# Row transfers on GpSimd without the memsets between them: a routed feed-forward, state-space, routed feed-forward layer on one core

## The chip, the core and the metric

The kernel runs on one core of a Trainium2 chip. Time is device microseconds for one execution. Before the change three runs took 1312.5, 1317.1 and 1319.66 us, with a median of 1317.1 us. The profile is of one further execution, which took 1298.57 us; its span from the first to the last instruction is 1296.8 us, at a mean granted TensorE clock of 0.887.

## What is computed

The input is 2 sequences of 2048 rows of 128 numbers, in float32. Three residual steps follow each other, each on a layer-normalised copy of the rows:

```python
x = x + 0.5 * ffn(layernorm(x))    # 32 experts, 4 per row, plus a shared part
x = x + attn(layernorm(x))         # a state-space scan over the 2048 rows
x = x + 0.5 * ffn(layernorm(x))    # the same experts again
```

In `ffn` a softmax over 32 logits picks the 4 best experts of each row. The row goes through those 4 (`down(silu(gate(row)) * up(row))`, all 128 x 128), the results are added with the weights of the softmax, and a shared block of the same form with 512 hidden units is added. In `attn` a state of 256 x 16 numbers per sequence is carried over the rows by `h = h * exp(dt * A) + dt * u * B`, and read out with `C`.

## The kernel before, in words

**Blocks and groups.** The 4096 rows are 8 blocks of 512. The first `ffn` treats the blocks in groups of 1, 1, 2 and 4 blocks, the last one in groups of 4, 2, 1 and 1 (`GROUPS`). The state-space part treats one block after another. One order of all operations mixes the three parts: state-space work of early blocks runs beside `ffn` work of other groups.

**Rows to their experts and back.** For a group, `mixture` works out a place for each (row, expert) pair, so that rows of one expert stand together. Then GpSimd sends the rows there: one indirect transfer (L916, 128 rows of 512 bytes) per tile of 128 rows and chosen expert, 16 for each block, from SBUF to a table `xs` in DRAM. SyncE loads the table in pieces of 4 x 128 rows (L1006) with the weights of their experts (L1018 or L1048); TensorE, ScalarE and VectorE apply the expert (L1066 to L1113), and the results go to a table `ys` in DRAM (L1117). GpSimd fetches them back by 4 indirect transfers for each tile (L1197) into one of the 4 buffers `yg`. ScalarE writes the weights on diagonals `dg` (L1222), TensorE adds the four up with them (`sum`, L1230), and VectorE adds the sum to `x` (L1241). Over all, 256 transfers go out (L916) and 256 come back (L1197).

**GpSimd's other work.** In the state-space part it makes the driving term of every state by one multiplication of 128 x 1024 (`hst`, L1456, 128 of them, into a ring of 4 buffers), which VectorE then scans (L1494), and three smaller operations for each half block (L1424 to L1426).

**What sets the order.** `ORDER` is a list of operation numbers written out by hand; `Plan.run` (L279) lists the operations in it and `Plan.emit` (L307) writes them out. PE, DVE, ACT and SP keep this order as it stands. GpSimd's instructions are tied by edges without a wait (`pool`, L394): everything but an outgoing transfer is tied to what went before; outgoing transfers are tied to the last instruction that is not one, and not to each other.

**The pad.** `Plan.run` counts how many transfers follow each other among GpSimd's operations (`row`; transfers are those with a `lag`). For the third and every later one of such a row it sets `o.pause`, and `emit` then writes a memset of a tile `pad`, which nobody reads, ahead of the transfer. The pad counts as an instruction that is not an outgoing transfer, so it also ties the transfers around it in order.

```python
    def pool(made, scatter=False):
        ins = made.ins
        if scatter:
            if behind[0] is not None:
                edge(behind[0], ins)
            behind[1].append(ins)
        else:
            for a in behind[1] or ([behind[0]] if behind[0] is not None else []):
                edge(a, ins)
            behind[0], behind[1] = ins, []
        return ins
    pad = const.tile([P, 256], BF16, tag="pad", name="pad")
    def pause():
        pool(nc.gpsimd.memset(pad, 0.0))
```

**Semaphores.** Each transfer on GpSimd signals its landing on one of eight semaphores in turn, so the ninth waits for the landing of the first.

Of the kernel before, what the change touches and what calls it, by code (L numbers as in the profile page):

```python
# [245 lines left out]
class Plan:  # L246
# [32 lines left out]
    def run(self):  # L279
        order, done, row = [], set(), 0  # L280
        for part in ORDER.split():
            first, _, last = part.partition("-")
            order += [self.ops[i] for i in range(int(first), int(last or first) + 1)]
        assert len(order) == len(self.ops)
        for o in order:


            assert o.deps <= done
            for b in o.bufs:
                if b.made:  # L290
                    continue
                line = self.made[b.ring]
                assert b.place is None or b.place == len(line)
                assert b.follow is None or (
                    b.follow.made and self.made[b.follow.ring][len(line)] is b.follow
                )
                k = len(line) - self.rings[b.ring]
                assert k < 0 or done.issuperset(line[k].ops)
                b.made = True
                line.append(b)  # L300
            done.add(o)
            if o.eng == "pool":
                row = row + 1 if o.lag else 0
                o.pause = row > 2
        return order

    def emit(self, order, pause):  # L307
# [1348 lines left out]
```

## Time and profile before

| what | value |
|---|---|
| median of 3 runs | 1317.1 us (1312.5 to 1319.66) |
| profiled execution | 1298.57 us, span 1296.8 us |
| PE matmul / weight loads busy | 977.2 us (75%) / 775.3 us (60%) |
| GpSimd busy | 976.6 us (75%), 1043 instructions |
| DVE / ACT busy | 822.4 us (63%) / 785.6 us (61%) |
| transfers out (L916) | 256, mean 0.975 to 0.989 us |
| DMA, mean | 175 GB/s |

The busy time of a GpSimd transfer is not the time in which its data move; that is done by the DMA engines afterwards. The row "software_dynamic" of the DMA queues holds these transfers: 16384 packets, 33.59 MB, that is 32 packets for each of the 512. An idle time that ends with "issue" is one for which the profile shows no wait.

### The profile page before, as it was taken

What the parts mean: (1) busy time and instruction counts of PE and PEld (TensorE: products, weight loads), DVE (VectorE), ACT (ScalarE), POOL (GpSimd) and SP (SyncE); (2) the same over time, 40 slices, a digit from 0 to 9 for tenths busy, and PEclk for the clock granted to TensorE, in tenths of its full rate; (3) what the DMA queues carried; (4) which work ended last, traced back from release to release, by engine and by line L of the source; (5) the groups of instructions that cost most, each with busy time, mean ns of one, the idle gap of its engine ahead of it and who ended that gap; (6) DMA issues with size and microseconds to landing.
All of it is one profiled execution on the core that took longest, in us unless ns stands there. A gap on an engine that the chain in (4) does not pass through costs nothing. (4 is left out here: it accounts for less than half of the span.)

```text
span 1296.8 us, 19377 instructions
## 1 busy us (share of the span) xinstructions
PE 977.2 (75%) x5823; PEld 775.3 (60%) x5848; DVE 822.4 (63%) x1643; ACT 785.6 (61%) x1532; POOL 976.6 (75%) x1043
## 2 busy tenths in 40 slices
PE   3778864778898978878668756767887889667776
PEld 2456654566777766565545445545767877666664
DVE  7543451146576999898989999998688633212221
ACT  4324333477789999677879735775678546333342
POOL 3874678088869685888989889989876867477586
PEclk9978987889999999777889776888999989879888
DMA  9768875678978464222232212332798968668632
GB/s 320 237 189 261 276 211 162 201 226 285 292 246 247 152 171 142 85 64 69 81 81 73 76 49 82 98 115 90 226 277 250 310 206 234 177 179 226 173 92 68
DMA packets 253514, 226.87 MB, mean 175 GB/s; under 512 B 24513, under 2 KB 218690, under 8 KB 253378
## 3 DMA queue, kind: packets, MB, share of 16 engines
q1 hardware_dynamic: 236994, 191.67, 48.6%
q0 software_dynamic: 16384, 33.59, 8.9%
q8 instruction: 60, 0.98, 0.3%
q14 instruction: 76, 0.62, 0.2%
HBM read 154.65 MB, written 70.52 MB: 174 GB/s over the span
## 5 line engine op out<-in xcount | busy, mean ns | idle before, releaser
L1456 POOL TENSOR_TENSOR hst<-dtu,bs 128x1024 f32<-128x1024 f32 x128 | 302.7, 2370 | 56.0 <-PE y L1271 15.9
L1197 POOL DMA_INDIRECT yg<-ys,idx x256 | 248.0, 969 | 114.5 <-PE sum L1230 52.1
L1076 PE MATMUL gu<-xT,wt 128*128 128x128 f32 x1536 | 220.3, 296 | 57.9 <-issue 13.6
L1076 PEld LDWEIGHTS gu<-xT,wt 128*128 128x128 f32 x1536 | 203.0, 207 | 93.6 <-issue 44.2
L916 POOL DMA_INDIRECT xs<-xn,idx x192 | 189.9, 989 | 88.8 <-issue 33.8
L1494 DVE TENSOR_TENSOR_SCAN hst<-da,st,hst 128x512 f32<-128x512 f32 x192 | 240.1, 1272 | 14.2 <-POOL hst L1456 5.9
L1094 DVE TENSOR_TENSOR h<-sgq,gu 128x256 f32<-128x256 f32 x192 | 77.9, 418 | 227.5 <-ACT sgq L1088 129.6
L1468 ACT ACTIVATE da<-dt,a 128x512 f32<-128x512 f32 x256 | 175.0, 690 | 73.2 <-DVE hst L1494 66.3
L1271 PEld LDWEIGHTS y<-ident,hst 128*128 128x128 f32 x1024 | 135.1, 157 | 77.0 <-issue 52.1
L1088 ACT ACTIVATE sgq<-gu 128x256 f32<-128x256 f32 x192 | 71.3, 384 | 162.9 <-PE gu L1076 81.7
L415 ACT ACT_TABLE_LOAD x130 | 166.8, 1283 | 4.1 <-PEq L1644 0.8
L1271 PE MATMUL y<-ident,hst 128*128 128x128 f32 x1024 | 152.3, 299 | 19.5 <-DVE hst L1507 18.1
L1507 DVE TENSOR_TENSOR hst<-hst,c 128x1024 f32<-128x1024 f32 x128 | 154.9, 1210 | 11.3 <-PE c L1480 3.6
L1104 PE MATMUL oq<-wt,h 128*128 128x128 f32 x768 | 110.4, 290 | 38.7 <-DVE h L1094 19.2
L1104 PEld LDWEIGHTS oq<-wt,h 128*128 128x128 f32 x768 | 100.2, 201 | 55.2 <-DVE h L1094 22.2
L409 POOL MEMSET pad<- 128x256 bf16 x336 | 110.5, 329 | 0.3
L1113 ACT COPY yq<-oq 128x512 f32<-128x512 f32 x96 | 55.7, 586 | 79.0 <-PE oq L1104 34.5
L1480 PE MATMUL c<-cm,pick 128*128 128x512 bf16 x103 | 44.4, 432 | 77.7 <-DVE hst L1507 72.6
L1230 PEld LDWEIGHTS sum<-yg,dg 128*128 128x128 f32 x512 | 71.6, 210 | 34.7 <-issue 12.9
L1230 PE MATMUL sum<-yg,dg 128*128 128x128 f32 x512 | 77.8, 300 | 17.3 <-issue 7.5
L1069 ACT COPY xT<-pt_x 128x512 f32<-128x512 f32 x96 | 55.7, 585 | 54.6 <-PE pt_x L1066 21.8
L1222 ACT ACTIVATE dg<-ident,wk 128x128 f32<-128x128 f32 x256 | 81.0, 394 | 10.4 <-PE sum L1230 10.4
(154 smaller groups left out, 1531.6 us busy)
## 6 DMA issues: line engine op xcount, KB each, us to landing
wt<-w_dram SPq DMA_DIRECT2D x256, 192.0 KB
bs<-bd SPq DMA_DIRECT2D x128, 256.0 KB
xs<-xs SPq DMA_DIRECT2D x96, 256.0 KB
ys<-yq SPq DMA_DIRECT2D x96, 256.0 KB
xs<-zero SPq DMA_DIRECT2D x52, 256.0 KB
wt<-in_gate_w SPq DMA_DIRECT2D x64, 128.0 KB
wt<-in_up_w SPq DMA_DIRECT2D x64, 128.0 KB
wt<-in_down_w SPq DMA_DIRECT2D x64, 128.0 KB
```

Source lines behind the costliest of these rows:

```text
L409: pool(nc.gpsimd.memset(pad, 0.0))
L415: nc.scalar.preload_act_table_set(name)
L916: nc.gpsimd.indirect_dma_start(out=xs_b.t, out_offset=bass.IndirectOffsetOnAxis(ap=route["idx"][:, i * TB + t, k : k + 1], axis=0), in_=xn ...
L1076: nc.tensor.matmul(gu.t[:, j, s, :], wt.t[:, s, j * H : (j + 1) * H], xT.t[:, s0 + s, :], start=True, stop=True,)
L1104: nc.tensor.matmul(o.t[:, s, :], h.t[:, s, :], wts[s // 2].t[:, s % 2, 2 * H :], start=True, stop=True,)
L1197: nc.gpsimd.indirect_dma_start(out=yg.t[:, k, :], out_offset=None, in_=ys_b.t, in_offset=bass.IndirectOffsetOnAxis(ap=route["idx"][:, i * ...
L1230: nc.tensor.matmul(sm_.t, dg.t[:, k, :], yg.t[:, k, :], start=(k == 0), stop=(k == TOPK - 1),)
L1271: nc.tensor.matmul(y[:, t, k * P : (k + 1) * P], src[:, k, t * P : (t + 1) * P], ident.t, is_transpose=True, start=start and k == 0 and t ...
L1456: nc.gpsimd.tensor_tensor(h.t[:, :, 1:], dtu.t, bs.t.unsqueeze(1).to_broadcast([P, ND, T]), ALU.mult)
L1468: nc.scalar.activation(da.t, dt.t[:, k, :], AF.Exp, scale=a_t.t[:, k, s : s + 1])
L1494: nc.vector.tensor_tensor_scan(h.t[:, k, 1:], da.t, h.t[:, k, 1:], 0.0 if ini else st_sb[:, k, s : s + 1], ALU.mult, ALU.add,)
L1507: nc.vector.tensor_tensor(h.t[:, :, :T], h.t[:, :, 1:], cb.t.unsqueeze(1).to_broadcast([P, ND, T]), ALU.mult,)
```

## The change

The third and later transfers of a row get no pad any more. Nothing else of the source is touched:

```diff
             if o.eng == "pool":
                 row = row + 1 if o.lag else 0
-                o.pause = row > 2
+                o.pause = False
         return order
```

336 memsets of 128 x 256 bf16 go. The instructions of the other four engines stay, in the same order. On GpSimd the sequence of the remaining instructions stays too, with two exceptions, both where outgoing transfers are no longer tied by a pad: nine of the four-block group now stand ahead of the branch of an earlier group (L1139) and not behind it, and among three transfers of two late groups one has moved to the front.

## The prediction

> **What bounds the kernel now.** I read the page first: engines, then groups.
>
> ```profile
> PE 977.2 (75%) x5823; PEld 775.3 (60%) x5848; DVE 822.4 (63%) x1643; ACT 785.6 (61%) x1532; POOL 976.6 (75%) x1043
> ...
> L1456 POOL TENSOR_TENSOR hst<-dtu,bs 128x1024 f32<-128x1024 f32 x128 | 302.7, 2370 | 56.0 <-PE y L1271 15.9
> L1197 POOL DMA_INDIRECT yg<-ys,idx x256 | 248.0, 969 | 114.5 <-PE sum L1230 52.1
> ...
> L916 POOL DMA_INDIRECT xs<-xn,idx x192 | 189.9, 989 | 88.8 <-issue 33.8
> ...
> L409 POOL MEMSET pad<- 128x256 bf16 x336 | 110.5, 329 | 0.3
> ```
>
> No engine is full. GpSimd's 977 us hold 110.5 us of pads, and the reader should notice the idle column: transfers have much, pads none. The windows by stage (columns: busy time and count of each engine, clock, DMA share, GB/s) show why the mean misleads.
>
> ```profile
> 20.00:230.00 210.00, 144.59 (x767) 108.34 (x765) 92.20 (x370) 74.35 (x151) 150.79 (x230) 0.87 0.73 231
> 230.00:1000.00 770.00, 602.79 (x3535) 469.54 (x3559) 631.96 (x976) 575.28 (x1057) 616.81 (x485) 0.89 0.50 152
> 1000.00:1297.00 297.00, 223.84 (x1503) 193.29 (x1503) 85.67 (x227) 127.99 (x305) 206.69 (x310) 0.90 0.65 186
> ```
>
> In the middle DVE (632 of 770) and GpSimd (617) hand the scan buffers to each other; at both ends PE, DMA and transfers alternate. Counted in GpSimd's timeline, 114, 73 and 149 pads lie in these three stages. Then the view of waits (columns: sum in us, times, longest), first GpSimd's, then SyncE's own:
>
> ```profile
> POOL yg L1197 <- PE sum L1230: 52.1, 17, 15.1
> ...
> POOL xs L916 <- ACTq L1139: 23.8, 1, 23.8
> ```
>
> ```profile
> SPq L1006 <- DMA xs<-xn,idx: 23.8, 2, 14.3
> ```
>
> So returning transfers wait 52.1 us for a free `yg`, and one outgoing group waits 23.8 us: slack that hides slower or faster transfers. But SyncE waits 23.8 us for rows to land, in two places (9.6 us near 45 us, and 14.3 us late in the middle): there transfers are on the path. Last, GpSimd's timeline of one row of transfers:
>
> ```profile
> 1017.75 1.01 POOL L916 DMA_INDIRECT xs<-xn,idx  x1 [0.16 <-issue]
> 1019.07 0.96 POOL L916 DMA_INDIRECT xs<-xn,idx  x1 [0.30 <-issue]
> 1020.02 0.33 POOL L409 MEMSET pad<- 128x256 bf16 x1
> 1020.52 0.97 POOL L916 DMA_INDIRECT xs<-xn,idx  x1 [0.17 <-issue]
> 1021.48 0.34 POOL L409 MEMSET pad<- 128x256 bf16 x1
> 1021.98 0.97 POOL L916 DMA_INDIRECT xs<-xn,idx  x1 [0.17 <-issue]
> ```
>
> Behind a pad a transfer starts 0.17 us after it; behind another transfer 0.30 us after it. With a pad one transfer costs 0.97 + 0.33 + 0.165 = 1.465 us; the second of a row, with none, 0.97 + 0.30 = 1.27 us. All 76 direct pairs have this gap. **No third transfer in a row without a pad is in the trace.**
>
> **The change, part by part.**
>
> *Removed: 336 pads.* If a third transfer behaves like a second, each saves 1.465 - 1.27 = 0.195 us of GpSimd: 336 x 0.195 = 65.5 us, not the 110.5 us of the pads' row, as the longer gap takes back 0.13 us.
>
> *How many of them are on the path.* Early stage: 14 pads in the first group's row (SyncE waits for its landing) and at most 16 in the return of the same group, which the state-space part needs; the other 84 end in waits of 23.8, 9.8 and 4.8 us. Middle: DVE and GpSimd share the bound, so I take half of 73, 36. Late: after the last wait at 1266 us 16 transfers run to 1288.7 us and the end follows at 1296.8 us: 16 pads; I add 24 for the last outgoing rows (1134 to 1166 us); the other 109 run into waits for `sum`. Sum: 30 + 36 + 40 = 106 of 336 on the path.
>
> *Added: a direct succession of three and more.* This is the unknown price; call the time from one to the next T.
> Lower end: the second of a row, 1.27 us. Then 106 x 0.195 = 21 us would be gained if nothing else were near; DVE in the middle and the sums at the end are, so I take half, 10 us.
> Upper end: a transfer that waits until the one ahead has left. I matched the packets of the software queue with the transfers, 32 each: from a transfer's start to the start of its last packet the shortest is 1.86 us, the median 2.92, the longest 6.71. T = 1.86 costs 0.395 us against the padded one: 106 x 0.395 = 42 us.
> Here a rule speaks against the change. The Trainium skill (DMA: Bandwidth & Descriptors, Anatomy of one DMA) gives each transfer from GpSimd a fixed 2.0 us plus bytes over 436 GB/s, mostly waiting for the write's receipt; for 64 KB an estimate of 2.15 us. By the row, 1.27 us from one to the next, the sum is a gain; by the rule, were it a rate, T = 2.15 costs 0.685 us: 106 x 0.685 = 73 us, and 109 x 0.685 - 57 us of late waits = 18 more, 91 us. The trace contradicts it as a rate for pairs: a second starts 1.27 us after the first, and in 182 of 512 transfers two or three earlier ones were not yet through. It stays an upper end for a longer row.
>
> *Which T.* The profile doesn't settle it. For a low T: the GpSimd stream already carries a transfer each 1.465 us beside a pad, so no resource with a plain rate can be slower than that. For a high T: the only direct pairs show 0.13 us more start delay than behind any other work, so one transfer leaves something for the next to wait for, and a pad covers it; transfers that start with three earlier ones open take 0.99 us in the mean (up to 1.45) against 0.966 with one open; and all pairs in the trace are followed by a pad or by 1.3 to 2.4 us of other work, in which a debt would be paid unseen. I take such a debt as likelier than none, and T between the sustained 1.465 and the shortest passage 1.86: 1.66 us, 0.195 us above the padded pace. It is a choice, not a row.
>
> *Moves.* Nine transfers pass a branch of GpSimd's queue, and three late ones change places. The branch has no busy row on GpSimd; another order of rows into one table moves a landing by one T at most: nothing, as they lie under the 30.1 us wait of L1424 in the early case and under waits of 0.8 to 1.4 us for `hst` in the late one; without that cover, 2 us. SyncE, PE, ACT and DVE keep their instructions, so nothing else passes a queue. No wait is added; behind a slow transfer stand GpSimd's next `hst` (DVE's scan waits for it) and the next transfers.
>
> *Sum.* 106 x 0.195 = 21 us on the path, the rest under waits. 1298.6 + 21 = 1319.6 us of the profiled kind; the runs' median stands 1317.1 / 1298.57 = 1.0143 above: 1338 us.
>
> **The rivals.**
>
> *The row goes on at 1.27 us* (0.28): the pads were only in the way. For: the 76 pairs, and the rate argument above. Against: nothing shows a third. -10 us, 1298.6 - 10 = 1288.6, times 1.0143: 1307 us; up to 1296 with all 21. It decides below T = 1.465, and ends on the faster side.
>
> *Serial transfers* (0.07): T at 2.15, by the sum above 91 us: 1410 us. Against: transfers with three open.
>
> *The eight semaphores become the wait.* The ninth waits for the first: 8 x 1.27 = 10.2 us, the longest passage is 6.7 us, so no wait; in the first burst, where the queue was never empty, eleven passed in 15.05 us, 1.37 each, so the queue itself would hold T at 1.37 there. This only shrinks the gain: 1312 us. It goes with the next case.
>
> *Hidden anyway* (0.10, with the one before): transfers end in waits; within 3 us of 1317.
>
> *A debt in a row*, my forecast: 0.55, T 1.52 to 1.9, 1324 to 1365 us.
>
> **How the numbers follow.** A measurement of this kernel can tell about 0.5% from no change (1310.5 to 1323.7 us). Faster: 0.20 of the 0.28. Same: 0.08 of it and the hidden 0.10, so 0.18. Slower: 0.55 + 0.07 = 0.62. Range: from the lower rival's middle less a few us, 1303, to somewhat above the debt's end, 1372; left out are the serial case and the best of the fast one. The likeliest case alone spans 1324 to 1365.
>
> **What would show it.** GpSimd's timeline: the third and later transfers of a row must start 0.5 us or more after the one ahead, or last 1.3 us and longer, against 0.30 and 0.97; groups L916 and L1197 must grow in busy or "issue" idle time; "PE sum" as releaser of L1197 must shrink below 52.1 us. If the third starts 0.30 us after the second, the first rival is right. If the slow spacing holds and the time stays, my 106 is wrong. If other engines' means move, contention did it.

## The result, and the profile after

| | before | after |
|---|---|---|
| median | 1317.42 us (1312.5 to 1319.66, 4 runs) | 1409.55 us (1407.92 to 1412.08, 4 runs) |
| profiled execution | 1298.57 us, span 1296.8 us | 1412.08 us, span 1410.3 us |
| mean TensorE clock | 0.887 | 0.851 |

The ratio is 1.071 [1.067, 1.074]: slower, by more than the range I gave.

This figure belongs to one kind of session. A session here is a set of runs on one chip, the kernel before among them. In five later sessions the kernel before took 1194 to 1200 us, in one 1316, in one 1305 and in two 1272 us. Within a session runs agree, so each ratio below compares runs of one session. Two chips (8 and 10) were met in both kinds, so the kind is not a fixed property of a chip. I call the sessions near 1195 us *prompt* and the others *late*, for a reason that the traces give below (the expectations on record say fast and slow kind, or fast and slow sessions).

First the page after: the engines, then the rows of the groups that the prediction named.

```profile
PE 1000.4 (71%) x5823; PEld 796.9 (57%) x5848; DVE 829.4 (59%) x1643; ACT 783.8 (56%) x1532; POOL 861.7 (61%) x707
...
L1197 POOL DMA_INDIRECT yg<-ys,idx x256 | 245.9, 960 | 217.0 <-PE sum L1230 89.2
L1456 POOL TENSOR_TENSOR hst<-dtu,bs 128x1024 f32<-128x1024 f32 x128 | 302.7, 2370 | 74.4 <-issue 20.0
L916 POOL DMA_INDIRECT xs<-xn,idx x192 | 187.2, 975 | 141.5 <-issue 56.8
```

GpSimd has shed its pads (976.6 to 861.7 us). No transfer got slower: 969 to 960 ns and 989 to 975 ns. What grew is the idle column, 114.5 to 217.0 and 88.8 to 141.5 us. GpSimd has less to do and waits more, for others. Now the windows by stage (columns as in the prediction). The first has the limits of before's first window, though the first `hst` starts only at 334 us here; the last begins a little ahead of the last `hst`, at 1093.7 us.

```profile
20.00:230.00 210.00, 128.54 (x619) 94.88 (x618) 80.64 (x339) 57.84 (x112) 83.22 (x87) 0.78 0.59 188
230.00:1080.00 850.00, 629.87 (x3694) 496.58 (x3715) 651.77 (x1015) 591.99 (x1098) 620.47 (x443) 0.86 0.49 149
1080.00:1410.00 330.00, 235.97 (x1493) 201.30 (x1495) 84.30 (x220) 126.09 (x303) 155.69 (x160) 0.85 0.58 167
```

The first row covers the same 210 us as the first row of before: PE did 619 matmuls there instead of 767, DVE 339 instructions instead of 370, and DMA's share fell from 0.73 to 0.59. Every engine stood still more. By milestones in the two traces, the first `hst` moved from 271.6 to 334.0 us (+62.4), the stretch from first to last `hst` from 743.6 to 759.7 (+16.1), and the rest from 281.6 to 316.6 (+35.0). The sum is 113.5 us, the difference of the spans. (That of the medians is 92 us, as before's profiled execution lies 1.4% below its median.)

The granted clock fell too, from 0.887 to 0.851. At that clock TensorE's matmuls were busy 23.2 us longer (977.2 to 1000.4 us), so the lower clock accounts for about a fifth of the 113.5 us at most, and the rest is waiting.

The timeline shows such a stand-still. These are lines of one row of 32 outgoing transfers after the change:

```profile
54.34 3.84 PE L976 MATMUL o<-w_all,hs 128*128 128x128 f32 x32 [0.26 <-DVE hs L965]
...
58.01 0.96 POOL L916 DMA_INDIRECT xs<-xn,idx  x1 [0.30 <-issue]
58.01 0.60 PE L1066 MATMUL pt_x<-ident,xs 128*128 128x128 f32 x4
...
58.45 1.02 PE L950 MATMUL gp<-xnT,w_all 128*128 128x512 f32 x2
59.28 0.96 POOL L916 DMA_INDIRECT xs<-xn,idx  x1 [0.31 <-issue]
60.54 0.96 POOL L916 DMA_INDIRECT xs<-xn,idx  x1 [0.30 <-issue]
61.81 0.95 POOL L916 DMA_INDIRECT xs<-xn,idx  x1 [0.30 <-issue]
...
72.66 0.69 DVE L988 SCALAR_TENSOR_TENSOR x<-o,x 128x512 f32<-128x512 f32 x1 [15.65 <-remote]
...
82.49 0.59 ACT L1069 COPY xT<-pt_x 128x512 f32<-128x512 f32 x1 [27.79 <-remote]
```

Read the starts of the transfers first: 58.01, 59.28, 60.54, 61.81. That is 1.265 us from one to the next, 0.30 us of gap and 0.96 of work, in the third as in the second and the twentieth. Then read who waits. TensorE's `o` ends at 54.34 + 3.84 = 58.18 us; VectorE's `x`, which reads it, starts at 72.66, 14.5 us later. `pt_x` ends at 58.61; ScalarE copies it at 82.49, 23.9 us later. The releaser is "remote": the profile found no instruction of this core that ended when the wait did. There is only one core in this program. TensorE itself had gone on, with `pt_x` at 58.01 and `gp` at 58.45. I read this as work that was done and whose signal came late; how far that is shown stands under "What stays open".

Here is the same pair of `o` and `x` in the changed kernel in a prompt session (e7_after):

```profile
44.22 3.84 PE L976 MATMUL o<-w_all,hs 128*128 128x128 f32 x32 [0.26 <-DVE hs L965]
...
48.09 0.69 DVE L988 SCALAR_TENSOR_TENSOR x<-o,x 128x512 f32<-128x512 f32 x1 [1.25 <-PE o L976]
```

`o` ends at 48.06, `x` starts 0.03 us later, and the releaser has its name.

The view of waits holds the sums, for the kernel after (first fence) and, of the same view, for the kernel before (second fence):

```profile
POOL yg L1197 <- PE sum L1230: 89.2, 16, 20.6
...
ACT sgq L1088 <- remote: 51.4, 7, 21.2
...
DVE x L988 <- remote: 41.6, 3, 18.9
...
ACT xT L1069 <- remote: 33.6, 3, 27.8
```

```profile
ACT sgq L1088 <- remote: 31.8, 12, 9.9
...
ACT xT L1069 <- remote: 14.4, 6, 6.3
...
DVE x L1241 <- remote: 11.5, 2, 9.4
...
DVE x L988 <- remote: 8.0, 1, 8.0
```

Over all lines "remote" makes 204.8 us after (30 waits, longest 27.8) and 86.4 us before (25 waits, longest 9.9). So the symptom stood in the profile of before, and I had read past it. (These sums run over several engines that can wait at once, so they are no share of the span.)

### The profile page after: what moved, and what is told of

Read it like the earlier page. It is cut to its first block, busy times and chain, and to the rows that moved or that the text cites. A ratio compares the mean times of both kernels' runs of the same rounds, so it can differ in the third digit from the quotient of the medians.

```text
span 1410.3 us, 19061 instructions
## 1 busy us (share of the span) xinstructions
PE 1000.4 (71%) x5823; PEld 796.9 (57%) x5848; DVE 829.4 (59%) x1643; ACT 783.8 (56%) x1532; POOL 861.7 (61%) x707
## 5 line engine op out<-in xcount | busy, mean ns | idle before, releaser
L1197 POOL DMA_INDIRECT yg<-ys,idx x256 | 245.9, 960 | 217.0 <-PE sum L1230 89.2
L1456 POOL TENSOR_TENSOR hst<-dtu,bs 128x1024 f32<-128x1024 f32 x128 | 302.7, 2370 | 74.4 <-issue 20.0
L916 POOL DMA_INDIRECT xs<-xn,idx x192 | 187.2, 975 | 141.5 <-issue 56.8
L1076 PE MATMUL gu<-xT,wt 128*128 128x128 f32 x1536 | 227.4, 302 | 64.7 <-issue 27.4
L1076 PEld LDWEIGHTS gu<-xT,wt 128*128 128x128 f32 x1536 | 210.0, 213 | 100.3 <-issue 46.2
L1094 DVE TENSOR_TENSOR h<-sgq,gu 128x256 f32<-128x256 f32 x192 | 77.8, 417 | 269.2 <-ACT sgq L1088 167.8
L1088 ACT ACTIVATE sgq<-gu 128x256 f32<-128x256 f32 x192 | 71.0, 383 | 172.7 <-PE gu L1076 84.4
L976 PE MATMUL o<-w_all,hs 128*128 128x128 f32 x512 | 77.6, 317 | 32.5 <-issue 32.2
L1066 PE MATMUL pt_x<-ident,xs 128*128 128x128 f32 x384 | 67.0, 303 | 46.4 <-issue 15.7
L976 PEld LDWEIGHTS o<-w_all,hs 128*128 128x128 f32 x512 | 75.0, 232 | 41.3 <-issue 39.6
```

What stands on the lines that cost most here:

```text
L916: nc.gpsimd.indirect_dma_start(out=xs_b.t, out_offset=bass.IndirectOffsetOnAxis(ap=route["idx"][:, i * TB + t, k : k + 1], axis=0), in_=xn ...
L976: nc.tensor.matmul(o.t[:, t, :], hs[c].t[:, t * P : (t + 1) * P], w_all[:, c, 2 * H :], start=(c == 0), stop=(c == NSH - 1),)
L1076: nc.tensor.matmul(gu.t[:, j, s, :], wt.t[:, s, j * H : (j + 1) * H], xT.t[:, s0 + s, :], start=True, stop=True,)
L1197: nc.gpsimd.indirect_dma_start(out=yg.t[:, k, :], out_offset=None, in_=ys_b.t, in_offset=bass.IndirectOffsetOnAxis(ap=route["idx"][:, i * ...
L1456: nc.gpsimd.tensor_tensor(h.t[:, :, 1:], dtu.t, bs.t.unsqueeze(1).to_broadcast([P, ND, T]), ALU.mult)
```

## The experiments

Beside each time I counted late signals. The trace records the updates of each engine's semaphore. For each update of TensorE's I took the time since the last TensorE instruction that raises it had ended, and call it late above 1 us. In every trace of a prompt session one or two at the most are late. VectorE's and ScalarE's updates, counted the same way, come after 0.01 us in the median in all traces, with at most 3 late ones.

In late sessions a part of these records is missing, of all three engines: 1077 against 1244 of TensorE's in before and e6_before, 1028 against 1336 of VectorE's, 944 against 1200 of ScalarE's, and 933 of TensorE's in e13_wide. So the counts there are rather low. The starts of the instructions do not depend on these records, and they say the same. With ScalarE free, its `sgq` (L1088) starts more than 1 us after the end of the `gu` that it reads 32 times of 192 in before, 17 times after the change and 22 times in e11_tiny, but once in e13_wide and never in e6_before and e7_after. VectorE's `h` (L1094) starts that late after ScalarE's `sgq` once or twice in each of the six. TensorE's signals are late, and ScalarE's to VectorE are not.

The spacing in the table is that of outgoing rows; returning transfers follow each other some 0.015 us closer.

| run | pad us, spacing of transfers us | before in its session | time us | ratio | late signals: number, sum, longest us |
|---|---|---|---|---|---|
| before, first comparison | 0.33, 1.465 | 1317 | | | 71, 168, 6.8 |
| changed, first comparison | none, 1.265 | 1317 | 1409.6 | 1.071 [1.067, 1.074] | 74, 235, 19.0 |
| e1_tiny | 0.12, 1.26 | 1200 | 1182.6 | 0.985 [0.980, 0.989] | 1, 4.5, 4.5 |
| e2_every4 | 0.33 at every 4th | 1200 | 1185.9 | 0.989 [0.986, 0.993] | 1, 4.2, 4.2 |
| e3_wide | 0.54, 1.67 | 1200 | 1241.3 | 1.035 [1.031, 1.040] | 1, 5.5, 5.5 |
| e4_enop | none, 1.265 | 1200 | 1184.0 | 0.986 [0.982, 0.990] | 1, 4.4, 4.4 |
| e5_after | none, 1.265 | 1194 | 1182.2 | 0.988 [0.981, 0.994] | 1, 3.7, 3.7 |
| e6_before | 0.33, 1.465 | 1197 | 1194.4 | | 2, 7.5, 5.5 |
| e7_after | none, 1.265 | 1197 | 1180.7 | 0.988 [0.985, 0.990] | 2, 5.6, 3.6 |
| e8_tiny | 0.12, 1.26 | 1197 | 1179.4 | 0.986 [0.983, 0.989] | 2, 6.6, 4.5 |
| e9_back | 0.33, only L1197 | 1197 | 1195.5 | 0.998 [0.996, 1.000] | 2, 8.0, 6.0 |
| e10_out | 0.33, only L916 | 1200 | 1181.2 | 0.985 [0.984, 0.987] | 1, 3.6, 3.6 |
| e11_tiny | 0.12, 1.26 | **1316** | 1423.2 | 1.082 [1.079, 1.085] | 86, 335, 29.1 |
| e12_wide | 0.54, 1.67 | 1195 | 1240.8 | 1.038 [1.027, 1.049] | 1, 5.5, 5.5 |
| e13_wide | 0.54, 1.67 | **1305** | 1244.8 | 0.954 [0.951, 0.957] | 4, 9.6, 5.5 |
| e14_mid | 0.43, 1.57 | **1272** | 1220.6 | 0.960 [0.955, 0.964] | 1, 5.5, 5.5 |
| e15_alt | 0.54 at every 2nd, 1.265 and 1.67 | **1272** | 1261.7 | 0.992 [0.990, 0.995] | 52, 116, 5.9 |
| e16_mid | 0.43, 1.57 | **1273** | 1221.2 | 0.960 [0.955, 0.966] | 3, 8.2, 5.6 |

My theory after the result was A, that it is the closeness of the transfers which holds the other engines up. The rivals were B, that an instruction of another kind between two transfers is what matters, and later D, that the signals' lateness comes from the chip and not from the kernel. The expectations on record also name C, that a late session is slower in everything, and E, which in e10_out is a form of A (no signal gets through before the row ends; the timeline above speaks against it, as `x` and `xT` start within the row) and in e11_tiny stands for B.

**First session: the pad's width and kind.** e1_tiny, e3_wide and e4_enop change what the pad is, e2_every4 how often it comes:

```diff
-    pad = const.tile([P, 256], BF16, tag="pad", name="pad")
+    pad = const.tile([P, 1], BF16, tag="pad", name="pad")       # e1_tiny
+    pad = const.tile([P, 512], BF16, tag="pad", name="pad")     # e3_wide
```
```diff
-                o.pause = row > 2
+                o.pause = row > 2 and row % 4 == 0              # e2_every4
```
```diff
-        pool(nc.gpsimd.memset(pad, 0.0))
+        pool(nc.gpsimd.engine_nop())                            # e4_enop
```

> The pad stays, but writes 1 column in place of 256, about 0.1 us by the row of one-column memsets, so that a transfer comes about 1.24 us after the one ahead, as close as without any pad (1.265 us). Theory A, closeness: TensorE's and the others' completion signals fall behind whenever transfers come closer than about 1.4 us, whatever stands between them. Then 1390 to 1420 us, as without pads. Theory B, kind: any other instruction of GpSimd between two transfers lets the signals through. Then 1295 to 1320 us.

> A pad of the old size ahead of every fourth transfer of a row alone. Mean distance (3 x 1.265 + 1.465) / 4 = 1.315 us. Theory A, closeness: the gap of one pad in four gives back a quarter of the 0.2 us, so most of the loss stays: 1360 to 1400 us. Theory B, kind: late signals begin some 8 transfers into a row, so one other instruction in four is enough: 1300 to 1325 us.

> Every pad writes 512 columns in place of 256: about 0.55 us in place of 0.33, a transfer each 1.7 us. Theory A, closeness: the trace of before has 71 of TensorE's signals more than 1 us late, 168 us in sum; with more room these get fewer, and time falls or stays within 1%: 1300 to 1325 us. Theory B, kind: no signal is earlier for it, and 336 x 0.23 = 77 us of GpSimd are added, a third on the path: 1335 to 1350 us.

> In place of each pad an empty instruction [...]that touches no memory. Theory A, closeness: as without pads, 1390 to 1420 us. Theory B, kind: if any instruction will do, 1295 to 1320 us; if only one that writes SBUF, 1390 us or more, and e1 tells the two apart.

None of them behaved like the first comparison: here the kernel before took 1200 us, each shortening gained 1 to 1.5% and the widening cost 3.5%. The empty instruction left the gap at 0.30 us and the spacing at 1.265, so e4_enop is the changed kernel in all but the order, and yet it was faster. Neither A nor B explains a gain; the session had to be asked about.

**The changed kernel again, and both kernels' profiles in prompt sessions.** e5_after and e7_after are the changed kernel, e6_before is the kernel before, e8_tiny repeats e1_tiny.

> The changed kernel once more, unaltered, as the experiments so far ran on a chip on which the kernel before takes 1200 us and shows no late signal, not 1317 us with 71 of them. Theory A, closeness, as a property of every chip: slower than the kernel before by 5 to 8%. Theory B, kind: the same, as nothing stands between the transfers. Theory D, the chip: signals fall behind on the first chip alone; where the kernel before takes 1200 us, the changed one takes about what the empty instructions gave, 0.985 of it, 1180 to 1190 us; where it takes 1317 us, about 1410 us.

> The kernel before, unaltered, for its profile on another chip than the one of the first comparison. Theory D (the chip of the first comparison delivers PE's signals late, other chips do not): on a chip where it takes about 1195 us, at most 2 of PE's signals come more than 1 us late (71 on the first chip, 168 us together), and the stages lie the difference of about 120 us shorter mostly where those delays were. If the chip is one like the first, about 1317 us and some 70 late signals. Theory C (the first chip is slower in everything, a lower clock say): the late signals stay as many, or there is another reason for 1317 against 1195 us, such as longer means of the same instructions.

> The changed kernel, unaltered, once more. Theory D: on a chip where the kernel before takes about 1195 us, a ratio of 0.98 to 0.995 as in the run before this; on one where it takes 1300 us or more, 1.05 to 1.09 with PE signals up to 20 us late inside the rows of transfers. A rival, that the first comparison was a disturbance of that hour and belongs to no chip: 0.98 to 0.995 wherever it runs.

> Pads of one element a row (0.12 us instead of 0.33), once more, beside the changed kernel on the same chip. On a chip of 1195 us: 0.98 to 0.99, not to be told from the changed kernel. On a chip like the first, theory A (what harms is the close succession): transfers 1.26 us apart as in the changed kernel, so also 1.05 to 1.09. Theory B (another kind of instruction between two transfers is what matters): within 1 per cent of the kernel before or faster.

The changed kernel is 1.2% faster than the kernel before there, twice, and the late signals are gone from both. Longer instructions are not the main difference between the kinds: `hst` takes 2.37 us and a transfer 0.97 us in both. The two profiles of the kernel before lie 104 us apart (1296.8 and 1192.6 us), 46 of them ahead of the first `hst`, 17 in the middle and 41 behind the last; TensorE's matmuls, at a clock of 0.887 against 0.903, make up 31.5 us of busy time (977.2 and 945.7 us), and the rest is waiting. Here are the stage windows of e6_before (first fence) and e7_after (second), with limits at the first and the last `hst`:

```profile
20.00:225.00 205.00, 163.38 (x932) 126.08 (x931) 99.33 (x385) 95.36 (x189) 161.84 (x240) 0.90 0.86 271
225.00:952.00 727.00, 579.34 (x3481) 458.12 (x3504) 637.63 (x979) 565.92 (x1038) 617.20 (x489) 0.89 0.52 158
952.00:1193.00 241.00, 196.98 (x1394) 170.16 (x1394) 74.55 (x210) 115.10 (x284) 192.57 (x297) 0.93 0.73 209
```

```profile
20.00:223.00 203.00, 162.63 (x937) 125.79 (x937) 98.79 (x384) 95.22 (x190) 125.36 (x127) 0.92 0.87 275
223.00:952.00 729.00, 575.42 (x3472) 453.46 (x3495) 640.84 (x978) 565.56 (x1038) 591.72 (x413) 0.90 0.52 158
952.00:1178.00 226.00, 192.67 (x1396) 168.05 (x1395) 74.62 (x210) 115.06 (x284) 143.74 (x150) 0.96 0.76 222
```

In the early stage DMA is the fullest (0.86 of the time busy, against 0.73 in the late session) and in the middle VectorE (638 of 727 us), and 36 and 25 us less of GpSimd change next to nothing there: -2.6 and +2.5 us by the exact milestones. In the last stage GpSimd was busy 193 of 241 us, and the stage ends 14.6 us earlier. That is the whole gain.

**Which half of the pads.** e9_back keeps pads in the returning rows only, e10_out in the outgoing rows only:

```diff
-                o.pause = row > 2
+                o.pause = row > 2 and o.fn.__name__ == "gather"     # e9_back
+                o.pause = row > 2 and o.fn.__name__ == "scatter"    # e10_out
```

> Pads stay in the rows that bring rows back (L1197), and are left out of the outgoing ones (L916). On a chip of 1195 us: 114+35 of the 336 pads or so are gone, most of those that I put on the path early; if the gain sits in the outgoing rows the ratio equals the changed kernel's, 0.985 to 0.992; if it sits in the returning rows (the last stage ends in them) 0.995 to 1.0. On a chip like the first: theory D puts the first stage's loss of 62 us into the outgoing rows, so 1.03 to 1.06.

> The other half of the run before: pads stay in the outgoing rows (L916) and are left out of the returning ones (L1197). Gain in the returning rows (the half with the outgoing pads left out gave 0.998): the whole of the changed kernel's gain, 0.985 to 0.991 where the kernel before takes about 1195 us, and the last stage shorter by about 14 us. Gain only when both are gone: 0.994 to 1.0. Where the kernel before takes 1300 us or more (theory E, made from the first two traces: a row without pads lets no signal of PE through until it ends): the loss of the returning rows alone, 1.02 to 1.05, and late PE signals beside returning rows only.

Without the 166 outgoing pads nothing changes (0.998), without the 170 returning ones the gain is whole (0.985). The rows that end the kernel are returning ones, and it is the last stage that gains: behind the last `hst` it takes 240.8 us in e6_before, 237.8 in e9_back, 227.2 in e10_out and 226.1 in e7_after.

**Late sessions: does the pace of GpSimd make the signals late?** e11_tiny and e13_wide are e1_tiny and e3_wide, met by late sessions; e12_wide met a prompt one and only repeats e3_wide.

> Pads of one element a row, on whatever chip it meets; asked of a chip on which the kernel before takes 1300 us or more and delivers PE's signals late. Theory A (closeness): GpSimd's transfers stand 1.26 us apart as without pads, the signals wait till the row's end, up to 20 us, and the time is 1.05 to 1.09 of the kernel before. Theory E (any instruction of another kind between two transfers opens a gap for the signals): the longest delay stays below 7 us as with the pads, 0.98 to 1.01. On a chip where the kernel before takes about 1195 us both say 0.98 to 0.99, and the run only repeats the earlier one.

> Pads of double width (0.54 us instead of 0.33, transfers 1.67 us apart), asked of a session of the slow kind (kernel before at about 1317 us). Theory A (the share of time that GpSimd's transfers leave free decides how soon PE's signals come through): fewer than 71 signals over 1 us late, their sum well below 168 us, and a time of 0.95 to 1.01, since what the pads cost (41 us in the fast kind of session) is won back from the delays. Rival, that a pad only has to be there and 0.33 us is enough: the delays stay at 168 us and the pads cost what they cost in the other sessions, 1.03 to 1.04. In a session of the fast kind (1195 us) both say 1.03 to 1.04, and it repeats the earlier run.

> Pads of double width once more (0.54 us, transfers 1.67 us apart), asked of a session of the slow kind (kernel before at about 1317 us). Theory A (the share of time that the transfers leave free decides the delay of PE's signals): fewer than 71 signals over 1 us late, their sum well below 168 us, 0.95 to 1.01. Rival, that a pad of 0.33 us is all that is needed: delays as with the pads of before, 1.03 to 1.04. In a session of the fast kind both say 1.03 to 1.04.

Theory B fell with e11_tiny, here its timeline:

```profile
56.57 3.84 PE L976 MATMUL o<-w_all,hs 128*128 128x128 f32 x32 [0.26 <-issue]
...
61.66 0.12 POOL L409 MEMSET pad<- 128x1 bf16 x1
61.97 0.96 POOL L916 DMA_INDIRECT xs<-xn,idx  x1 [0.19 <-issue]
...
90.82 0.69 DVE L988 SCALAR_TENSOR_TENSOR x<-o,x 128x512 f32<-128x512 f32 x1 [31.61 <-remote]
```

All 336 pads are there, but short, and the spacing is that of the changed kernel. `o` ends at 60.41, and `x` starts 30.4 us later, as the row ends. A memset between the transfers is no help; its length is. e11_tiny also keeps GpSimd's order of before, so the transfers that changed places are not the reason of the loss. Its longest delay, 29.1 us, lies beyond the 20 us that A gave. e13_wide shows the other side, in a late session too:

```profile
44.98 3.84 PE L976 MATMUL o<-w_all,hs 128*128 128x128 f32 x32 [0.26 <-issue]
...
48.85 0.69 DVE L988 SCALAR_TENSOR_TENSOR x<-o,x 128x512 f32<-128x512 f32 x1 [1.25 <-PE o L976]
...
71.19 0.97 POOL L916 DMA_INDIRECT xs<-xn,idx  x1 [0.17 <-issue]
72.15 0.55 POOL L409 MEMSET pad<- 128x512 bf16 x1
72.86 0.97 POOL L916 DMA_INDIRECT xs<-xn,idx  x1 [0.17 <-issue]
```

Transfers 1.67 us apart, `x` 0.03 us after `o`, not one "remote" wait in the whole trace, and 1244.8 us, where prompt sessions gave 1241.3 and 1240.8 us for the same kernel. The granted clock is the same in both kinds then (0.893 in e12_wide and e13_wide), so the lower clock of the other late runs comes with the stand-stills and not with the session. With such pads the kind of session makes hardly any difference, and a *wider* pad is 4.6% faster there while it is 3.5% slower in a prompt session. D, that the chip alone does it, is too little: session and pace do it together.

**Where the edge lies.** e14_mid and e16_mid have pads of 384 elements a row, e15_alt has wide pads at every second place:

```diff
+    pad = const.tile([P, 384], BF16, tag="pad", name="pad")     # e14_mid, e16_mid
```
```diff
+    pad = const.tile([P, 512], BF16, tag="pad", name="pad")     # e15_alt
+                o.pause = row > 2 and row % 2 == 1              # e15_alt
```

> Pads of one and a half widths (0.43 us, transfers 1.57 us apart). Slow session: if the delays shrink in step with the gap, some 80 us of late signals and a ratio of about 0.97; if there is an edge below 1.57 us, under 20 us of late signals and 0.93 to 0.95 (that is, below the double width's 0.954). Fast session: half way between the kernel before and the double width, 1.015 to 1.02.

> Pads of double width (0.54 us) after every second transfer of a row only, so that transfers stand 1.265 and 1.67 us apart in turn, 1.47 us in the mean as in the kernel before. Slow session, if the mean share decides: delays as before, some 170 us, 0.99 to 1.01. If the length of each gap decides: fewer than 30 us, 0.92 to 0.96. If two close transfers are enough to hold the signals up: as bad as without pads, above 1.03. Fast session: 1.0, since the same pad time is on GpSimd.

> Pads of one and a half widths (0.43 us, transfers 1.57 us apart) in one more session. If GpSimd's pace there lies past the edge from which PE's signals are held up: 1213 to 1226 us in any session, that is a ratio of 1.015 to 1.025 where the kernel before takes about 1195 us, 0.92 to 0.935 where it takes about 1315 us, and no more than 5 signals over 1 us late. If the edge lies elsewhere in a slower session: up to 80 us of late signals there, and 0.95 to 0.98.

They met sessions of a milder late kind (1272 us before). At 1.57 us at most 3 signals are more than 1 us late and the time is 1221 us, twice; no "remote" wait is left in either trace. Small delays stay: 20 updates of TensorE's in each come 0.5 us late or more, and 12 in e13_wide, against 3 in e6_before. The ratio of 0.960 lies in neither range that I gave for e14_mid, as these ranges were made for a session of 1317 us; the few late signals speak for the edge. These two sessions have no trace of the kernel before. If it has late signals there, as its 1272 us suggest, the edge lies between 1.465 and 1.57 us. e15_alt, with about the mean spacing of before, keeps 52 late signals and is 0.8% faster than before: a long gap at every second place does not do the work of a sufficient one at each. Its time is what I expected if the mean spacing decides (0.99 to 1.01), but its 116 us of late signals, where I expected 170, can't be set against a count of their own session. e14_mid beats the kernel before in late sessions of this kind; the changed kernel was run in none of them. In a prompt session e14_mid was not run; from e3_wide's cost (41 us for 0.21 us more in each pad) I estimate for 0.10 us more some 20 us, 1.7% slower than before.

## Why the prediction was wrong

It said slower, 1338 us; it is slower, and the reason was another one. Point by point:

- **The step that failed: "T between the sustained 1.465 and the shortest passage 1.86: 1.66 us", a debt in GpSimd's own row.** There is no debt. In rows without pads a transfer goes out each 1.265 us and comes back each 1.25 us, in late and prompt sessions alike, for rows of up to 32. My mark for this was the third transfer's start; it says that the first rival, "the row goes on at 1.27 us", was right on GpSimd. I had read the 0.13 us of longer start delay as a sign of more to come; it is simply the same for each. My other sign, 0.99 us for transfers that start with three earlier ones open against 0.966 with one, left out those with none open: they take 1.01 us in the mean in the same trace.
- **The extra loss had no term in the sum.** I wrote that the other engines keep their instructions, "so nothing else passes a queue", and counted only what waits for GpSimd. In late sessions TensorE's signals got through less the closer the transfers stood (9.6, 168 and 335 us of lateness in sum at 1.67, 1.465 and 1.26 us: e13_wide, before and e11_tiny), and the loss arose on DVE, ACT and the queues that wait for TensorE. My debt was to cost 21 us on the path; it cost none, and what the sum left out came to +113.5 us in that trace plus the gain hidden in it. "Remote" waits grew by 118 us, which is of that size, though waits of several engines overlap. Slower came out right, by luck.
- **What I did not read.** I looked at the waits of GpSimd and SyncE only. The lines of DVE and ACT in the same view held 86.4 us of "remote", of which neither kernel has any in a prompt session.
- **The on-path count of 106 pads.** In prompt sessions the early 30 and the middle 36 were worth nothing (-2.6 and +2.5 us) and the late 40, at 0.195 us 7.8 us, were worth 14.6 us. My halved -10 us for the first rival, a ratio of 0.992, was thus near 0.988 [0.985, 0.990] by two errors that offset each other.
- **"PE sum" must shrink below 52.1 us.** It grew to 89.2 us in the late session, as `sum` itself was late, and in a pair of prompt traces it went from 14.6 to 28.7: faster transfers reach the occupied `yg` sooner. The direction was wrong for either theory.
- **Serial transfers, and the rule of a fixed 2.0 us** (the Trainium skill, DMA: Bandwidth & Descriptors, Anatomy of one DMA): rows of 32 at 1.265 us rule it out as a rate. That this rival's 1410 us is the measured time to the microsecond is chance. **The eight semaphores** never held a row back: the gap stays at 0.30 us beyond the ninth transfer, in the first burst too, where I had put 1.37 us from one to the next.
- **"If other engines' means move, contention did it."** `hst` does not move (2370 ns both times). One engine's pace held up others all the same, through late signals, which no mean of an instruction shows; whether the two contend for something is not shown. That mark was badly chosen.

**What stays open.** Why sessions differ, what the signals share with GpSimd's transfers, and why TensorE's are late and the others' are not, no run here shows. The traces of late sessions lack a part of the update records of all engines; whether that loss has the same cause as the late signals, or the recording itself takes part, is untested. The ends of matmuls are modelled in the profile, so I cannot strictly tell a late signal from a late true end of the matmul. That TensorE starts its next groups at once (58.01 and 58.45 us above) speaks for the signal; the waiting engines see the same. The unaltered changed kernel met a late session once only; e11_tiny, at the same spacing, is the second case.

## What to carry to other kernels

An instruction that computes nothing may be a spacer: before taking it out, ask what it lets pass, and look for waits without a releaser ("remote" on a single core) on *all* engines beside it. Price an edit on one engine also by what its new pace does to its neighbours: here the same edit is worth -1.2% or +7%, according to whether signals were already late before. When a kernel's time has two levels on the same program, judge an edit in both: the pad of 0.43 us gave 1221 us in late sessions, where the kernel before took 1272 us.

## What the runs showed of the hardware that I had not expected

- Indirect transfers of 128 rows on GpSimd follow each other at a steady 1.265 us out and 1.25 us back in rows of up to 32, also with a memset of 0.12 us or an empty instruction between them.
- In some sessions TensorE's signals reach the waiting engines up to 29 us late while such transfers stand 1.265 us apart, up to 7 us at 1.465, and at 1.57 and 1.67 us no later than the 5.5 us that a prompt session has too. In the trace of before none of the delayed updates (0.5 us or more) falls between 0.35 and 0.68 us after the start of a transfer; the others lie in its first 0.35 us, its last 0.3 us, in the pads or behind a row. In the trace after, 84 of 109 come over 0.4 us after the latest transfer has ended, where the gap within a row is 0.30 us.
- One program, with the same means of GpSimd's instructions, takes 1195 us in some sessions and 1317 us in others. GpSimd's pads of 0.54 us bring the two to 1241 and 1245 us.
